# Where three of four value projections stand in the two attention stages with sixteen small heads

## The chip, the core and the metric

The kernel runs on one core of a Trainium2 chip. The core has a matrix engine (PE, or TensorE; the loading of its weights is shown as PEld), a vector engine (DVE), a scalar engine with tables for functions such as the exponential (ACT), a general engine (POOL) and a queue that issues transfers (SP). The engines run side by side, each through its own list of instructions in order, and wait for one another by semaphores. TensorE's clock is not constant: the profile shows which share of full speed was granted at each moment, called PEclk or granted clock. Matmuls write to PSUM, which this kernel divides into banks of 512 columns.

The metric is the time of one execution on the device in microseconds (us). Before the change it was 3802.96 us, the median of three runs (3797.84 to 3808.43).

## The reference

The program is a stack of four blocks on one activation of 2048 tokens by 128 features. Each block is half a feed-forward, an attention, and half a feed-forward again, all with a layer norm before and a residual after. The change touches the attentions of the second and the third block, which have sixteen heads of eight features and no causal mask; the third differs by a rotation of queries and keys:

```python
qkv = qkv.reshape(B, N, 3, HEADS, HEAD_DIM)        # 16 heads of 8
q, k, v = (qkv[:, :, 0], qkv[:, :, 1], qkv[:, :, 2])
q = q * scale
attn = jnp.einsum('bnhd,bmhd->bhnm', q, k)
attn = jax.nn.softmax(attn, axis=-1)
out = jnp.einsum('bhnm,bmhd->bnhd', attn, v)
```

With one batch of 2048 tokens each head has 2048 by 2048 scores. The values v of a token are its normed features times a matrix of 128 by 128.

## The kernel before, in words

**Tiling.** The 2048 tokens are four chunks (NC = 4) of 512 columns (CH), a chunk is four tiles (TC = 4) of 128. The function `packed` (line 1296) does one attention with small heads. The sixteen heads are four groups g of four; an iteration is a pair of a group and a chunk of queries, so there are sixteen, in the order group by group. The four heads of a group lie on the 128 partitions, 32 for each, so that a score product has 32 rows, and a value product 32 columns of output.

**Two passes.** The function `flash` (line 970) runs two streams. `stream_a` is the first pass: for an iteration it multiplies queries by all keys (line 1069) and takes the maximum of each row on DVE (line 1087, two heads at a time). It goes over the keys in two halves (`pi`, called `pair` in the hook): the chunks 0 and 1, then 2 and 3; in each over the four query tiles `r`. `stream_b` is the second pass: for each of the sixteen key tiles `kt` of 128 and each of the four heads it computes the scores again with the maximum folded in (line 1190), takes the exponential on ACT (line 1199), and multiplies by the values (line 1136) into one bank `pv`. The first pass of the first iteration runs alone; after that the two are interleaved in proportion to their columns, the first pass about one iteration ahead. The order on PE in these streams is fixed in the program by `tc.keep_in_program_order`; what is issued without it (projections, copies) is placed by a scheduler, earlier where it can, and `tc.high_priority()` lets it go ahead of others.

**Projections.** `front(c)` (line 1316) norms and turns a chunk and leaves it, turned, in `vall[c]`. `queries_or_keys(n, c)` (line 1325) makes keys (n = 1) or queries (n = 0) with three products of 512 columns (`product`, lines 227 to 229), cast on ACT and completed on DVE. `values(c)` (line 1334) multiplies the four tiles of `vall[c]` by the value matrix into one bank and copies that back into `vall[c]` on ACT (line 1341). It takes its bank from `bank()`, which has three, shared with the scores of the second pass and with the other projections.

**Stacks.** `stack_q` and `stack_k` put queries and keys of a group and chunk into their partitions by three DMAs each (line 1379), issued by SP. `stack_v(g, c)` (line 1401) copies the four heads' values of a chunk into the tile `v` of the group on DVE (line 1403); the value products read that tile. Key tile `kt` needs chunk `kt // 4`.

**Who calls what, and when.** `hook(n, pair, r)` is called by the first pass ahead of each query tile. For the first iteration it makes the last keys (pair 0, tile 0), and in the second half of the keys (`pair == 1`) it calls `values(r)` and `stack_v(0, r)` for r = 0 to 3, and at r = 2 stacks the queries of the second iteration. `poll(at)` is called in the second pass ahead of each of its steps, with the iteration and key tile at hand (-1 and 0 before the first). It stacks keys and values of group 1 at its first call, and later groups when an iteration has been passed. In the program's list for PE the scheduler has put the value projections of the second block's attention ahead of the first maximum's matmul, and those of the third block's among the first ones.

Of the kernel before, what the change touches and what calls it, by code (L numbers as in the profile page):

```python
# [21 lines left out]
NC = 4  # L22
# [42 lines left out]
def tile_macaron(ctx: ExitStack, tc: tile.TileContext, a: dict, out: bass.AP, stages=STAGES):  # L65
    nc = tc.nc
# [6 lines left out]
    def bank(name="bank"):  # L73
        return psum.tile([P, CH], F32, name=name, tag="s2", bufs=3)
# [1221 lines left out]
    def packed(io, early, hd, causal, scale, project, w, wv, wo, bias=None):  # L1296
# [4 lines left out]
        n_groups = C // (4 * hd)  # L1301
# [3 lines left out]
        def slots(v):  # L1305
            return v[:, : NT * 4 * slot].rearrange("p (t j d) -> p t j d", j=4, d=slot)
# [24 lines left out]
            last_of[n, c] = nc.vector.tensor_tensor(l, src, h.bitcast(F32), ALU.subtract)  # L1331
            parts[c][n] = h, l

        def values(c):
            ps = bank().rearrange("p (i c) -> p i c", i=TC)
            f = vall[c].rearrange("p i c -> p (i c)")
            for i in range(TC):
                nc.tensor.matmul(
                    ps[:, i], f[:, i * P : (i + 1) * P], wv, start=True, stop=True
                )  # L1340
            nc.scalar.copy(vall[c], ps)

        for c in range(1 if causal else NC - 1):
            while not io.ready(c):
                yield 0
            front(c)
            yield 1.5
            queries_or_keys(1, c)
            if c == 0:
                queries_or_keys(0, c)  # L1350
            yield 1.5
            if causal:
                values(c)
        yield True

        with tc.tile_pool(name="att", bufs=1) as pool, tc.tile_pool(name="far", bufs=1) as far:
# [27 lines left out]
            def stack_k(g, c):  # L1384
                t = kms[(g * NC + c) % n_km if not causal else g * NC + c]
                h, l = parts[c][1]
                for i in range(nq):
                    rows_of(t[:, i, :], (h, l, h), (g * nq + i) * per * hd)
                km[g, c] = t
# [11 lines left out]
            def stack_v(g, c):  # L1401
                vt[g] = vts[g % 2]
                nc.vector.tensor_copy(
                    slots(vt[g])[:, c * TC : (c + 1) * TC, :, :hd],
                    vall[c][:, :, g * 4 * hd : (g + 1) * 4 * hd].rearrange(
                        "p i (j d) -> p i j d", j=4
                    ),
                )
# [9 lines left out]
            def steps_of(i):  # L1418

                if not x_parts[i]:  # L1420
                    xn = layer_norm(i, False)
                    yield
                    front(i, xn)
                    yield
                    queries_or_keys(1, i)
                    if causal:
                        queries_or_keys(0, i)
                        yield
                        values(i)
                        yield  # L1430
                for g in range(2 if causal else 1):
                    stack_k(g, i)
                    if causal:
                        stack_v(g, i)
                        queue(its.index((g, i)))
                        yield

            def onward(c):

                if keyed[0] > c:  # L1440
                    return False
                if not making:
                    making.append(steps_of(keyed[0]))
                if next(making[0], True):
                    making.pop()
                    keyed[0] += 1
                return True
# [3 lines left out]
            def ensure(c):  # L1451
                while onward(c):
                    pass

            def queue(n):

                if n < len(its) and its[n] not in qt:
                    c = its[n][1]
                    if not parts[c][0]:
                        queries_or_keys(0, c)  # L1460
                    stack_q(*its[n])
# [8 lines left out]
            def hook(n, pair, r):  # L1470

                if causal:
                    if its[n][1] + 1 < NC:
                        onward(its[n][1] + 1)
                    return None
                if n == 0:
                    if pair == 0 and r == 0:
                        with tc.high_priority():
                            ensure(NC - 1)
                    if pair == 1:  # L1480
                        values(r)
                        stack_v(0, r)
                        if r == 2:
                            with tc.high_priority():
                                queue(1)
                elif pair == 1 and r == 2:
                    queue(n + 1)

                if n == 0 and (pair, r) in ((0, 1), (1, 3)):
                    return last_of[(1, NC - 1) if pair == 0 else (0, 1)]  # L1490
# [14 lines left out]
                    fill(t[:, NT * 4 * slot :], 1.0, True)  # L1505

            grown = [0 if not causal else n_groups]

            def poll(at):

                if causal:
                    return
                n, kt = at
                g = grown[0] + 1
                if g < n_groups and (g < 2 or n >= NC * (g - 1)):
                    for c in range(NC):
                        stack_k(g, c)
                        stack_v(g, c)
                    grown[0] = g
# [45 lines left out]
            def finish(n, pv, after, pe):  # L1565
# [32 lines left out]
                def out_b(oT):  # L1598
# [11 lines left out]

            io.upcoming()
            flash(io, pool, early, its, 4, causal, scale, s1, s2, pv_mm, put_max, begin, finish, poll,
                  leads=leads, hook=hook, flush=not causal, order=(2, 3, 0, 1) if per == 4 else (1, 0, 3, 2))

    def projections(pool, wqk):
# [24 lines left out]
    def attn0(io, k, w, early):  # L1640
        w, project = w
        yield from packed(io, early, 16, True, 16.0**-0.5, project, w, 2 * C, 3 * C)
# [5 lines left out]
    def attn1(io, k, w, early):  # L1648
        w, project = w
        yield from packed(io, early, 8, False, 8.0**-0.5, project, w, 2 * C, 3 * C, row("b_proj"))  # L1650
# [40 lines left out]
    def attn2(io, k, w, early):  # L1691
        w, project = w
        yield from packed(io, early, 8, False, 8.0**-0.5, project, w, 4 * C, 5 * C)
# [591 lines left out]
```

## Time and profile before

One execution was profiled. It took 3781.83 us, with a span of 3779.9 us from its first to its last instruction; the three runs shown above were executed without a profile.

| | busy us | share of the span |
|---|---|---|
| PE | 3450.8 | 91% |
| PEld | 1847.3 | 49% |
| DVE | 2873.0 | 76% |
| ACT | 2035.4 | 54% |
| POOL | 827.9 | 22% |

A busy engine is one with an instruction under way, whatever its clock. By windows around the two stages:

| from, to (us) | what runs | PE busy | DVE busy | ACT busy | granted clock |
|---|---|---|---|---|---|
| 802 to 866 | second block: front, and maxima of the first iteration | 37.54 | 52.62 | 7.41 | 0.58 |
| 866 to 915 | its second pass begins | 47.32 | 27.68 | 26.22 | 0.50 |
| 915 to 1600 | the rest of it | 666.96 | 617.37 | 555.12 | 1.00 |
| 1735 to 1782 | third block: maxima of the first iteration | 32.77 | 45.82 | 3.48 | 0.61 |
| 1782 to 1833 | its second pass begins | 49.32 | 29.78 | 26.47 | 0.50 |
| 1833 to 2450 | the rest of it | 593.71 | 567.36 | 531.78 | 0.98 |

In the profile a matmul of `values` stands as two passes of 128 columns each (line 1338: 32 passes for the sixteen matmuls of a stage). They start between 812.5 and 818.7 us in the second block and between 1735.4 and 1742.7 us in the third.

### The profile page before, as it was taken

To read this page: it belongs to the slowest core of one execution; us is meant where nothing else is said; L and a number is where in the kernel's file an instruction comes from. 1 tells how busy PE (TensorE), PEld (TensorE's weight loads), DVE (VectorE), ACT (ScalarE), POOL (GpSimd) and SP (SyncE) were. 2 spreads that over 40 slices of the span, in tenths; PEclk is the share of its full clock that TensorE was granted. 3 is DMA by queue.
4 is the path that set the end of the run, shared out by engine and by line. 5 is a ranking of instruction groups with operands and counts; after the bars stand their busy time and mean duration, and the time that the engine had idled before them with its cause. 6 is when DMAs were issued, how large, how long until landed. Compare 5 with 4: busy or idle time off the path is not lost. (4 is left out here: it accounts for less than half of the span.)

```text
span 3779.9 us, 64635 instructions
## 1 busy us (share of the span) xinstructions
PE 3450.8 (91%) x25325; PEld 1847.3 (49%) x25325; DVE 2873.0 (76%) x4793; ACT 2035.4 (54%) x3838; POOL 827.9 (22%) x830
## 2 busy tenths in 40 slices
PE   7689988979999999996999999988899999999999
PEld 5543356853333333883333333376444444444458
DVE  6578556767999997668799999654677877788862
ACT  3246722315888888332688888732333444444442
POOL 1511124010000000111000000142555445533341
PEclk9779989976999999996799999898899999999999
DMA  3410023010000000102000000012443333221010
GB/s 104 94 48 19 27 69 92 1 26 5 14 10 14 8 3 1 35 7 64 9 14 6 16 5 4 12 49 75 137 147 111 99 108 97 89 63 52 24 34 12
DMA packets 124689, 170.18 MB, mean 45 GB/s; under 512 B 25120, under 2 KB 52514, under 8 KB 124384
## 3 DMA queue, kind: packets, MB, share of 16 engines
q1 hardware_dynamic: 121824, 160.80, 14.0%
q0 software_dynamic: 2560, 5.25, 0.9%
q8 instruction: 199, 3.26, 0.4%
q14 instruction: 106, 0.87, 0.1%
HBM read 101.25 MB, written 45.87 MB: 39 GB/s over the span
## 5 line engine op out<-in xcount | busy, mean ns | idle before, releaser
L1087 DVE TENSOR_REDUCE mp<-s 128x2 f32<-128x1024 f32 (+3 forms) x1440 | 1628.1, 1181 | 115.3 <-PE s L1069 84.8
L1199 ACT ACTIVATE pt<-s 128x512 f32<-128x512 f32 (+1 forms) x2368 | 1220.4, 602 | 250.5 <-PE s L1190 155.5
L1190 PE MATMUL s<-q,km 32*128 32x512 f32 (+2 forms) x2368 | 751.9, 504 | 24.2 <-ACT pt L1199 14.2
L1136 PE MATMUL pv<-pt,v 128*32 128x256 f32 (+1 forms) x8568 | 752.6, 424 | 22.9 <-ACT ov L1568 11.3
L1069 PE MATMUL s<-km,qt 32*128 32x512 f32 (+3 forms) x2368 | 634.0, 519 | 57.5 <-DVE mp L1087 36.1
L1190 PEld LDWEIGHTS s<-q,km 32*128 32x128 f32 (+1 forms) x2368 | 329.7, 188 | 549.3 <-issue 360.6
L1179 ACT ACTIVATE pt<-s 128x512 f32<-128x512 f32 (+3 forms) x640 | 306.1, 530 | 357.0 <-PE s L1171 213.8
L143 POOL TENSOR_TENSOR rs<-rs,minus_half 128x4 f32<-128x4 f32 x56 | 57.7, 1030 | 1555.9 <-DVE rs L142 1555.0
L1136 PEld LDWEIGHTS pv<-pt,v 128*32 128x32 f32 x8568 | 171.1, 109 | 325.0 <-issue 151.8
L1984 DVE TENSOR_TENSOR sum<-sum,pt 128x512 f32<-128x512 f32 (+3 forms) x328 | 259.3, 806 | 89.0 <-ACT pt L1179 87.7
L1171 PE MATMUL s<-q,k 64*128 64x512 f32 (+3 forms) x1920 | 299.9, 403 | 16.3 <-ACT pt L1179 10.8
L1136 PE MATMUL pv<-pt,latv 128*64 128x512 f32 (+3 forms) x1280 | 310.7, 565 | 1.3 <-ACT pt L1179 1.3
L1984 POOL TENSOR_TENSOR sum<-sum,pt 128x512 f32<-128x512 f32 (+1 forms) x200 | 264.8, 1324 | 182.7 <-ACT pt L1179 179.6
L1069 PEld LDWEIGHTS s<-km,qt 32*128 32x128 f32 (+1 forms) x2368 | 241.0, 195 | 119.4 <-DVE mp L1087 79.2
L1171 PEld LDWEIGHTS s<-q,k 64*128 64x128 f32 x1920 | 161.7, 188 | 226.7 <-issue 138.3
L715 ACT ACTIVATE sg<-pg 128x1024 f32<-128x1024 f32 x72 | 73.9, 1026 | 174.3 <-PE pg L229 155.3
L1069 PE MATMUL s<-k,q 64*128 64x512 f32 (+3 forms) x640 | 132.4, 428 | 19.4 <-DVE mp L1087 19.0
L1782 DVE TENSOR_TENSOR rot<-rot,tab 128x512 f32<-128x512 f32 x128 | 87.7, 685 | 74.0 <-PE rot L229 39.4
L725 PEld LDWEIGHTS pd<-l1d,h 128*128 128x128 f32 x1152 | 139.3, 192 | 5.6
L725 PE MATMUL pd<-l1d,h 128*128 128x128 f32 x1152 | 140.1, 275 | 0.0
L717 DVE TENSOR_TENSOR h<-pu,sg 128x1024 f32<-128x1024 f32 x72 | 87.9, 1220 | 60.5 <-PE pu L229 55.5
L1171 PE MATMUL s<-q,two 64*128 64x512 f32 (+3 forms) x640 | 128.3, 369 | 0.0
(575 smaller groups left out, 4682.1 us busy)
## 6 DMA issues: line engine op xcount, KB each, us to landing
tab<-in_l3rope SPq DMA_DIRECT2D x66, 256.0 KB
q<-q SPq DMA_DIRECT2D x32, 512.0 KB
k<-k SPq DMA_DIRECT2D x32, 512.0 KB
l0e<-in_l0e SPq DMA_DIRECT2D x32, 256.0 KB
q<-h SPq DMA_DIRECT2D x32, 256.0 KB
q<-rot SPq DMA_DIRECT2D x32, 256.0 KB
k<-h SPq DMA_DIRECT2D x32, 256.0 KB
k<-rot SPq DMA_DIRECT2D x32, 256.0 KB
```

The source lines that it names most:

```text
L715: nc.scalar.activation(sg, pg, AF.Silu)
L717: nc.vector.tensor_tensor(h.rearrange("p m n -> p (m n)"), pu, sg, ALU.mult)
L725: nc.tensor.matmul(pd[:, i, :], h[:, m, i * P : (i + 1) * P], wd[:, m, :], start=m == 0, stop=m == 1,)
L1069: pe(nc.tensor.matmul(ps[:, o : o + w], lhsT, rhs[:, :w], start=True, stop=not masked))
L1087: ins = nc.vector.tensor_reduce(mp[:, r, j0 : j0 + 2, kc], both[:, :, :w], AX.X, ALU.max,)
L1136: i = pe(nc.tensor.matmul(pv[out_rows, lo:hi], lhsT, pts[j][:, lo:hi], start=kt == 0, stop=kt == nt - 1 and hi == CH))
L1171: pe(nc.tensor.matmul(outs[j][:, c0:], lhsT, rhs[:, c0:], start=i == 0, stop=i == len(terms[0]) - 1 and not diag,))
L1179: ex = nc.scalar.activation(pts[j][:, c0:], outs[j][:, c0:], AF.Exp, scale=scale)
L1190: pe(nc.tensor.matmul(ps[:, c0:], lhsT, rhs[:, c0:], start=i == 0, stop=i == len(terms) - 1 and (tiled or not diag),))
L1199: ex = nc.scalar.activation(pt[:, c0:], ps[:, c0:], AF.Exp, scale=scale)
L1782: nc.vector.tensor_tensor(t.bitcast(F32), ps, halves["tabs"][i], ALU.mult)
L1984: eng.tensor_tensor(t[:, c0:], other[:, c0:], pts[j][:, c0:], ALU.add)
```

## The change

`hook` calls `values` and `stack_v` for chunk 0 alone. `poll` gets a new condition: the first time that it is called in the first iteration with a key tile above 0, it makes the values of chunks 1, 2 and 3 and stacks them for group 0, with high priority, and with the matmuls kept in the program's order (`values` has a new argument for that). A list `dense` notes that this is done, and group 1 is stacked only afterwards. The causal attention of the first block goes through the same functions, but its calls of `values` are as before.

```diff
-        def values(c):
+        def values(c, keep=lambda ins: ins):
...
-                nc.tensor.matmul(
+                keep(nc.tensor.matmul(
                     ps[:, i], f[:, i * P : (i + 1) * P], wv, start=True, stop=True
-                )
+                ))
...
                     if pair == 1:
-                        values(r)
-                        stack_v(0, r)
+                        if r == 0:
+                            values(0)
+                            stack_v(0, 0)
...
             grown = [0 if not causal else n_groups]
+            dense = []
...
                 n, kt = at
+                if not dense and n == 0 and kt > 0:
+
+                    dense.append(n)
+                    with tc.high_priority():
+                        for c in range(1, NC):
+                            values(c, tc.keep_in_program_order)
+                            stack_v(0, c)
                 g = grown[0] + 1
-                if g < n_groups and (g < 2 or n >= NC * (g - 1)):
+                if g < n_groups and dense and (g < 2 or n >= NC * (g - 1)):
```

In the program's lists of instructions the twelve matmuls of chunks 1 to 3 then stand, in both stages, in one piece among the first score products of key tile 1: after one of them and a pair of the second iteration's maxima, and ahead of the next score product and of the first value product. Their three copies stand on ACT between exponentials, and six copies into `v` (chunks 1 to 3 for groups 0 and 1) on DVE between maxima. One matmul of chunk 0 stands behind the Q projection in the second block's front where it stood ahead of it. The DMAs of the keys and queries are the same; two of those at the start change places.

## What the change does to the time: a prediction

> **What bounds the kernel now.** I read the page's busy shares first (PE 91% of the span, DVE 76%), then the slices in time, then the two stages with sixteen heads by windows, then single instructions there. The change touches only those stages (about 802 to 1600 us and 1700 to 2450 us), so I need what limits them, and where. In the slices, compare the busy TensorE with the clock it was granted: in slices 10 and 20 PE is busy nine tenths while PEclk has 9 and 7.
>
> ```profile
> PE   7689988979999999996999999988899999999999
> PEclk9779989976999999996799999898899999999999
> ```
>
> The windows of the first of the two stages split that up. Columns: stretch, its length, busy us (instructions) of PE, PEld, DVE, ACT, POOL, then the granted clock.
>
> ```profile
> 820.00:860.00 40.00, 25.32 (x66) 9.22 (x66) 36.09 (x33) 0.00 (x0) 0.00 (x0) 0.53 0.13 33
> 866.00:880.00 14.00, 12.32 (x62) 3.95 (x60) 7.92 (x7) 9.06 (x16) 0.00 (x0) 0.50 0.00 0
> 880.00:890.00 10.00, 10.00 (x64) 3.02 (x60) 5.43 (x5) 4.14 (x8) 0.00 (x0) 0.50 0.01 2
> 890.00:900.00 10.00, 10.00 (x58) 3.10 (x52) 5.83 (x6) 5.10 (x10) 0.00 (x0) 0.50 0.00 1
> 900.00:920.00 20.00, 19.99 (x136) 6.48 (x135) 13.31 (x12) 12.25 (x24) 0.00 (x0) 0.63 0.04 11
> 920.00:960.00 40.00, 39.19 (x396) 15.63 (x396) 38.07 (x39) 35.14 (x68) 0.00 (x0) 1.00 0.05 11
> ```
>
> Three regimes: until about 866 the maxima of the first iteration run alone and DVE is full (36.09 of 40); from 866 the second pass runs on a full PE at **half clock**, with DVE and ACT about half idle; from about 915 the clock is 1.0 and PE and DVE are both full. The pace is read from the value products (L1136), two halves for each key tile:
>
> ```profile
> 883.35 1.08 PE L1136 MATMUL pv<-pt,v 128*32 128x256 f32 x8
> 885.09 1.08 PE L1136 MATMUL pv<-pt,v 128*32 128x256 f32 x8
> 887.62 1.08 PE L1136 MATMUL pv<-pt,v 128*32 128x256 f32 x8
> ...
> 915.45 0.64 PE L1136 MATMUL pv<-pt,v 128*32 128x256 f32 x8
> 916.74 0.64 PE L1136 MATMUL pv<-pt,v 128*32 128x256 f32 x8
> 917.75 0.64 PE L1136 MATMUL pv<-pt,v 128*32 128x256 f32 x8
> ```
>
> At half clock a key tile takes 887.62 - 883.35 = 4.27 us, at full clock 917.75 - 915.45 = 2.30 us. The second stage repeats it: clock 0.50 from 1748, full pace from 1833.19. So for some 45 us of each stage the bound is the granted clock, and the question is **what raises it**. In this trace every step of the clock lies a whole number of 3.413 us apart from every other (805.7, 815.95, 822.8, 914.9), so it is decided window by window. In the second pass windows full of score and value products are refused twelve times; the rise at 914.9 comes one window after a Q projection (L227 to L229, 128 rows, 908.23 to 909.9), the one at 1833.1 two windows after another (1824.33 to 1827.2). After both, the halves follow at 1.74 us steadily, where 1.74 and 2.53 us alternated before. And just such value projections as are moved here have raised it, before the maxima:
>
> ```profile
> 812.00:813.00 1.00, 1.00 (x4) 0.91 (x5) 0.57 (x1) 0.40 (x1) 0.00 (x0) 0.50 0.00 0
> 813.00:814.00 1.00, 1.00 (x6) 1.00 (x6) 0.00 (x0) 0.19 (x1) 0.00 (x0) 0.50 0.00 0
> 814.00:815.00 1.00, 1.00 (x4) 0.81 (x4) 0.00 (x0) 0.13 (x1) 0.00 (x0) 0.50 0.00 0
> 815.00:816.00 1.00, 1.00 (x7) 1.00 (x6) 0.52 (x1) 0.94 (x2) 0.00 (x0) 0.53 0.00 0
> 816.00:817.00 1.00, 1.00 (x10) 1.00 (x10) 0.44 (x3) 0.42 (x1) 0.00 (x0) 1.00 0.25 61
> ```
>
> Within the window 812.5 to 815.95 lie two K products and some twelve value passes; at its end the clock is 1.0. In the second stage the window 1734.1 to 1737.5, mostly value passes, ends in a rise too.
>
> **What is removed from the front.** Per stage twelve of the sixteen matmuls of `values` go; the trace has two passes for each, so 24 passes, with 3 copies on ACT (585 ns each, L1341) and 6 on DVE (L1403, median 218 ns: three for group 0, three for group 1, whose stacking now waits for the new place too). In the first stage 14 passes (814.63 to 816.74) stand ahead of the Q projection of chunk 1 on PE. That is on the path, through SP's queue: the rest of the first query tile (`qt<-qL`, issued at 820.81) is queued behind the tile of chunk 1, which waits for the cast of that projection (ACT, 817.72 to 818.30); the first maximum's matmul starts at 823.16. With the passes gone the cast ends about 2.07 us earlier (816.23). But SP had issued two of the key copies (815.48, 816.20) while it waited, and in the new order they come after it, before `qt<-qL`: from 816.25, six issues of 0.47 to 0.6 us put it at 819.8, **1.0 us earlier**. The other key and query DMAs keep their order. In the second stage DVE carries the front from 1735.49 to 1783: the hole at 1737.85 to 1738.70, in which the reduction waits for a score matmul behind value passes (0.85 us), goes, and about 0.9 us of DVE copies between the maxima: **1.7 us**.
>
> **What is added at the second pass.** The new order of PE puts the 24 passes after the second iteration's score pair at 869.49 (before), ahead of the fourth score matmul of key tile 1 and the first value product. Each projection takes one of the three banks that the scores use, and waits for the exponential that frees it; ACT runs its first exponentials from 868.35 at some 0.51 us each, so the third is done at 869.9 and the fifth at 870.9, before their banks are wanted. Queued behind the burst on PE are a score matmul, which waits for the first projection's ACT copy (done while the other two run), and the value product. On ACT the three copies stand ahead of the next exponential, on DVE the six copies ahead of the next maxima, for up to 0.6 us after the burst, when their next inputs are not there. I cost the DVE copies at 0.6 us a stage, half of 6 x 0.2: nothing if the idle DVE hides them (5.4 busy of 10 before), 1.2 if DVE is already the bound.
>
> The price of the burst: cold, six passes took 1.14 us (812.49 to 813.63), 0.19 each, so 24 take 4.6 us; at full clock some 0.10 each (14 passes in 2.11 us, the clock rising among them). By the windows above, about 1 us of value passes in a window besides score products should carry it over: the rise then falls 1 to 4.4 us after the burst's start, as the window happens to lie; I take 2.6 us (14 passes cold, 10 warm): **3.6 us**. Ends: 2.9 us; and 4.6 us plus up to 3.3 us at the cold pace of 3.48 us a tile, if a second window is needed (another 1.1 us lost).
>
> **What it brings.** First stage, from 869.98 to 915.01, 45.0 us before: the value product of key tile 0 (2.58 us cold, 1.4 warm), 19 halves, one Q projection. At full clock: 1.4 + 19 x 1.15 = 21.85 + Q 0.8 (its warm length at 816.74) + burst 3.6 = 27.65. Gain **17.4 us**. Second stage, 1786.08 to 1833.19, 47.1 us: the same 19 halves, a projection of six products (1.55 warm, 1739.06 to 1740.6): 1.4 + 21.85 + 1.55 + 3.6 = 28.4. Gain **18.7 us**. Sum: 17.4 + 18.7 + 1.0 + 1.7 - 1.2 = 37.6, say **37 us**. What is late next is DVE, 98% full at full clock; that is in the 2.30 us.
>
> [...]
>
> **Against the median.** The profiled execution took 3781.83 us (span 3779.9), the median of three is 3802.96, and none was under 3797.84. The sum is made within the profile: 3745. I keep the 21 us between the two, since nothing here says where they lie: 3766. If the timed runs find their rise later than the profiled one, the gain is larger.
>
> **Rivals.**
> 1. *One stage only.* The burst lifts one stage, and in the other the windows cut it so that it counts too little, or a quiet window drops the clock again (as once at 1874, for one window). For: windows with half a projection were refused (908.1, 1822.9). Against: these held 128x512 products, and the window at 812.5 rose with less. Gain about 37 - 19 = 18: 3785.
> 2. *The clock doesn't rise at the burst* and rises at the Q projection as before: front -2.7, burst +9.1, copies +1.2, about +8: 3811; less where the steady 1.74 us comes earlier (3.48 against 4.27 a tile). With that it is no measurable change.
> 3. *Slower: the old trigger is lost as well.* The rise in the second pass is narrow: windows nearly as full as the one at 911.5 were refused (887.6). If the burst fails and shifts the streams so that the Q projection no longer tips it, the clock stays at half until the next iteration's projection, 16 tiles x 1.97 us = 31 us in a stage: 3803 + 8 + 31 = 3842. It decides when the clock is still 0.50 after the projection of query chunk 2.
>
> That the moves aren't made is excluded by the order of the instructions; the rest of the program keeps its order but for one table load and one rotation in the front of the second stage.
>
> **Chances.** Forecast 0.74 (3748 to 3778 by the ends above), one stage only 0.12, no rise 0.08, lost trigger 0.06. 0.3% is 11.4 us, what a measurement of this kernel can tell from no change. Faster: 0.74 + 0.12 = 0.86; same 0.08; slower 0.06. The range 3742 to 3800 takes in the first two cases, and at the low end timed runs in which the old rise was later.
>
> **What would show it.** In the profile after: granted clock 1.0 within about 5 us of the twelve projections in both stages, the halves of L1136 1.15 us apart from the second key tile on, the first maximum's matmul 1 us earlier in the first stage, no L1341 between the maxima of the second. It is wrong if the clock stays 0.50 through the burst, or falls again within the first iteration.

## The result, and the profile after

The changed kernel takes 3765.32 us (median of five, 3762.61 to 3769.46), the kernel before 3802.96: 0.990 of it, with a 95% interval of 0.9881 to 0.9919. In a later comparison it was 0.9913 (0.9892 to 0.9934). The profiled execution took 3769.46 us. The forecast of 3766 was met; the sum behind it was not, as the stages show.

The slices of the page, busy TensorE and granted clock (against the two rows of before: slice 10 has PEclk 7 for 6, where the prediction's text has 9, and slice 20 has 9 for 7):

```profile
PE   7679987978999999996999999888999999999989
PEclk9779988987999999996999999998899999999999
```

The first stage by windows (length, then busy us of PE, PEld, DVE, ACT, POOL, granted clock). This execution reaches the stage 13 us later than the first profile did; its second pass begins at about 882:

```profile
820.00:880.00 60.00, 34.89 (x97) 15.07 (x97) 49.56 (x49) 3.59 (x8) 5.33 (x10) 0.53 0.12 32
882.00:887.00 5.00, 4.59 (x20) 3.95 (x21) 2.58 (x4) 2.91 (x6) 0.00 (x0) 0.50 0.01 3
887.00:914.00 27.00, 24.18 (x217) 9.00 (x217) 20.71 (x21) 19.14 (x37) 0.00 (x0) 1.00 0.00 1
914.00:960.00 46.00, 45.22 (x450) 18.28 (x449) 43.22 (x43) 40.54 (x78) 0.00 (x0) 1.00 0.06 14
```

The half clock ends at 887.2, some 5 us into the second pass, where it lasted 47 us before; in the second stage it ends at 1795.2. But from 887 to 914 PE is busy only 24.18 of 27 us, DVE 20.71, ACT 19.14: at full clock no engine is full. PE in order of time shows the burst and what follows:

```profile
883.63 4.66 PE L1338 MATMUL bank<-l1a,vall 128*128 128x128 f32 x24
...
888.64 1.06 PE L1136 MATMUL pv<-pt,v 128*32 128x512 f32 x8
...
892.32 0.64 PE L1136 MATMUL pv<-pt,v 128*32 128x256 f32 x8
892.89 0.50 PE L1190 MATMUL s<-q,km 32*128 32x512 f32 x1
892.90 0.50 PE L1069 MATMUL s<-km,qt 32*128 32x512 f32 x2
893.69 0.50 PE L1190 MATMUL s<-q,km 32*128 32x512 f32 x1 [0.29 <-ACT pt L1199]
894.18 0.64 PE L1136 MATMUL pv<-pt,v 128*32 128x256 f32 x8
...
895.18 0.64 PE L1136 MATMUL pv<-pt,v 128*32 128x256 f32 x8
```

The burst starts at 883.63, and the clock rises 3.6 us later. After it the halves follow at 1.86 and 1.01 us by turns (892.32, 894.18, 895.18), so 2.86 us for a key tile and not 2.30; in front of every second one a score matmul waits for an exponential. That lasts for eight tiles, until the Q projection at 913.7. The waits of ACT in that time (engine and line, for whom, us in total, times, longest), first after, then in the kernel before from 873 to 908:

```profile
ACT pt L1199 <- PE pv L1136: 6.4, 8, 0.8
```

```profile
ACT pt L1199 <- PE pv L1136: 17.6, 8, 2.2
```

The same eight waits stand in both (and in the second stage, 6.3 us after and 17.6 before): an exponential waits for a **value product**. It writes a tile `pt`, and waits until an older one has been read. No row shown in the prediction had this wait, and its sum has no term for it.

By stages, the time from the first exponential of the second pass to the last value product:

| | before, two profiles | after, two profiles |
|---|---|---|
| second block | 649.1, 650.3 | 640.3, 639.1 |
| third block | 663.4, 665.3 | 648.7, 653.5 |
| sum | 1312.5, 1315.6 | 1289.0, 1292.5 |

The stages gain 23 us on average, where the prediction had 36.1 without the fronts and 34.9 with its reserve for DVE.

### The profile page after: what moved, and what is told of

The parts are those of the page before. It is cut to its first block, busy times and chain, and to the rows that moved or that the text cites. A ratio compares the mean times of both kernels' runs of the same rounds, so it can differ in the third digit from the quotient of the medians.

```text
span 3767.7 us, 64628 instructions
## 1 busy us (share of the span) xinstructions
PE 3420.8 (91%) x25325; PEld 1846.5 (49%) x25325; DVE 2870.9 (76%) x4793; ACT 2036.2 (54%) x3838; POOL 828.8 (22%) x830
## 5 line engine op out<-in xcount | busy, mean ns | idle before, releaser
L1190 PE MATMUL s<-q,km 32*128 32x512 f32 (+2 forms) x2368 | 733.6, 491 | 28.6 <-ACT pt L1199 18.7
L1136 PE MATMUL pv<-pt,v 128*32 128x256 f32 (+1 forms) x8568 | 730.9, 413 | 22.9 <-ACT ov L1577 11.2
L1069 PE MATMUL s<-km,qt 32*128 32x512 f32 (+3 forms) x2368 | 620.0, 507 | 61.1 <-DVE mp L1087 37.1
```

The costliest lines, as they stand in the source:

```text
L1069: pe(nc.tensor.matmul(ps[:, o : o + w], lhsT, rhs[:, :w], start=True, stop=not masked))
L1136: i = pe(nc.tensor.matmul(pv[out_rows, lo:hi], lhsT, pts[j][:, lo:hi], start=kt == 0, stop=kt == nt - 1 and hi == CH))
L1190: pe(nc.tensor.matmul(ps[:, c0:], lhsT, rhs[:, c0:], start=i == 0, stop=i == len(terms) - 1 and (tiled or not diag),))
```

## The experiments

The theories when they began. **A**: the burst of full-array products raises the clock, and that is the gain. **B**: the emptier fronts and the moved copies are the gain. Later, from the waits of ACT, **C**: the second pass is short of tiles for the exponentials. Ratios are to the kernel before on the same chip.

**The kernel before, again.** No edit.

> The kernel before, unchanged, with a second profile and five more timed runs. Theory A (the half clock at the start of the second passes is what the change removes, and its length differs from run to run): the times spread between 3782 and 3808, the longer ones have a lower mean granted clock, and the profile has half-clock stretches of at least 85 us around the start of each second pass. Rival (the half-clock stretch is the same in every run, and the 21 us between the profiled run and the median are elsewhere): the stretches end with the Q projection of the third query chunk again, and times don't follow the mean clock.

Ratio 1.000 (0.9985 to 1.0015); 22 executions from 3779.59 to 3819.32 us, with the mean clock going against the time (correlation -0.93): 0.938 in the shortest, 0.927 in the longest. So times do follow the clock, as A has it. But the second profile has its stretches of half clock in the same places, ending after the Q projections, and took 3799.9 us. It differs from the first profile ahead of the touched stages: its first attention begins at 193.7 us against 185.3, and from that attention's end to the next one's start it is another 6.7 us. These 15 us go with the chip, not the kernel: on the two chips where the kernel before has a median of 3781 or 3786 that start is at 184 to 189 us and the second stretch 363 us long, on the two with 3803 or 3804 it is 193 to 196 and 369 to 371, for every version run here. Part of it is a pause of TensorE among the gathered products, 5.0 us in the one feed-forward and 6.5 in the other, which the first profile doesn't have; what causes it is open. The record doesn't name the chip of the first profile, but by its start it goes with the faster two. So most of the 21 us between that profile and the median was probably the chip, and keeping them in the forecast was right.

**The burst alone.** The values stay in the front; the same twelve products are made a second time at the second key tile and not read:

```diff
+                if not burst and n == 0 and kt > 0:
+                    burst.append(n)
+                    with tc.high_priority():
+                        for c in range(1, NC):
+                            ps = bank("burst")
+                            for i in range(TC):
+                                tc.keep_in_program_order(nc.tensor.matmul(
+                                    ps[:, i * P : (i + 1) * P], vall[c][:, i, :], wv, start=True, stop=True
+                                ))
```

> The value projections stay in the front as before; a copy of the burst alone is added at the second key tile: twelve matmuls of 128x128 whose result nobody reads. Theory A (the burst raises the clock, and the clock is the gain): granted clock 1.0 within 5 us of the burst in both stages, about 34 us faster than before (the 37 less the 2.7 of the fronts), so 3765 to 3775. Rival B (the emptier fronts and the moved copies are the gain): slower than before by the burst, 6 to 9 us, near 3810.

Ratio 0.9932 (0.9912 to 0.9952), 28 us faster than before, though it does more. Its windows around the burst, which starts at 885.99:

```profile
884.00:889.00 5.00, 4.31 (x20) 3.59 (x19) 2.45 (x2) 2.67 (x6) 0.00 (x0) 0.50 0.00 0
889.00:915.00 26.00, 23.44 (x217) 8.61 (x216) 19.19 (x17) 17.12 (x33) 0.00 (x0) 1.00 0.00 1
```

The clock is 1.00 from 889, and B is out as the main cause: most of the gain needs nothing moved.

**A burst of another kind.** As above, with products of 32 rows in place of the full ones:

```diff
-                                    ps[:, i * P : (i + 1) * P], vall[c][:, i, :], wv, start=True, stop=True
+                                    ps, qt[its[0]][rows(0), 0, i * P : (i + 1) * P],
+                                    km[0, 0][rows(0), 0, :], start=True, stop=True
```

> The kernel before with a burst of the same place and about the same length (12 products of 512 columns, some 5 us at half clock), but of 32 rows by 128 columns each, one after another, result unread. Theory A (what counts in a window is how much of the array works): the clock stays 0.50 through the burst and comes with the Q projection as before; the time is that of before plus the two bursts, 3803 to 3815. Rival (a window in which TensorE has no gap is enough, whatever it does): the clock rises within 5 us of the burst as in the run with full products, 3770 to 3780.

Ratio 1.0013 (0.9999 to 1.0028). PE and its windows:

```profile
869.09 4.10 PE L1521 MATMUL burst<-km,qt 32*128 32x512 f32 x9
872.57 0.79 PE L1190 MATMUL s<-q,km 32*128 32x512 f32 x1
872.99 1.48 PE L1521 MATMUL burst<-km,qt 32*128 32x512 f32 x3
```

```profile
868.00:875.00 7.00, 6.99 (x21) 4.56 (x25) 1.81 (x2) 2.38 (x5) 0.00 (x0) 0.50 0.00 0
875.00:911.00 36.00, 35.69 (x204) 10.34 (x196) 20.27 (x17) 16.72 (x33) 0.00 (x0) 0.50 0.00 1
```

PE is busy 6.99 of 7 us, for longer than the full burst, and the clock stays at 0.50 for 46 us more, to 920.6. So a PE without gaps was not enough here: behind 4.37 us of full products the clock was 1.00 from 889, behind 5.58 us of 32-row products it was 0.50. The two bursts also differ in width (128 columns at a time against 512), but behind products of 128 rows and 512 columns it rose too, at 871.1 in the early Q projections below.

**Not in one piece.** Eight passes each at key tiles 1, 5 and 9; group 1 is stacked after the third:

```diff
-                if not dense and n == 0 and kt > 0:
+                c = len(dense) + 1
+                if c < NC and n == 0 and kt >= 4 * c - 3:
...
```

> The same move, but a chunk at a time: eight passes at key tile 1, eight at key tile 5, eight at key tile 9. Theory A with the weight I put on a projection (1 us of value passes in a window is enough): the first eight passes, 1.5 us, raise the clock in about half of the windows' positions, so between the kernels: 3765 to 3790. Theory A2 (a window must be nearly full of projections): the clock stays 0.50 until the Q projection and the time is near that of before, 3795 to 3810. Rival B (front): as after, 3765.

Ratio 0.997 (0.9953 to 0.9988), 13 executions from 3777.75 to 3803.20, so between the kernels and wide. In its one profile the eight passes at 884.03 sufficed in the first stage (clock up at 887.8); in the second those at 1792.45, 1811.32 and 1830.39 did not, and it came at 1840.1, after the Q projection. Three windows of the clock, found from its steps, hold of the value passes (length, then busy us of PE and PEld with L1338 alone, granted clock):

```profile
884.37:887.78 3.41, 1.74 (x8) 1.44 (x7) 0.50 0.02 5
1792.31:1795.73 3.42, 2.08 (x8) 1.78 (x8) 0.50 0.02 5
1829.86:1833.27 3.41, 2.07 (x8) 1.78 (x8) 0.50 0.00 0
```

```profile
1796.00:1836.00 40.00, 39.75 (x221) 14.04 (x213) 21.28 (x21) 17.95 (x34) 0.00 (x0) 0.50 0.00 0
```

The first of these windows ended in a rise; the other two did not, though all eight passes lay in them. So the clock rose behind a burst of 2.1 us once and not the other times; what decided it is open. Behind the piece of 24 passes it rose in both stages of the profile after (4.66 and 5.28 us of passes, up at 887.2 and 1795.2), and in the first stages of the burst alone (4.37 us, 1.00 from 889), of the earlier burst (4.63 us from 880.97, with the next score product at 0.50 us) and of the version with the Q projections below (0.91 on average from 872 to 880). My "about 1 us of value passes in a window is enough" is refuted at 1792.

**A tile earlier.** The burst ahead of the last scores of key tile 0:

```diff
-                if not dense and n == 0 and kt > 0:
+                if not dense and n == 0:
```

> The burst one key tile earlier, ahead of the last scores of key tile 0. Theory A: the clock rises some 2 us earlier, and what runs between is at full speed 1 to 2 us a stage sooner: 2 to 4 us faster than after. Rival (the burst then holds up the first exponentials and their values, and the start waits): the same as after or up to 4 us slower.

Ratio 0.9919 (0.9899 to 0.9939), where the change has 0.990 and 0.9913: no gain that can be told. The second passes take 639.0 and 653.8 us, as in the two profiles after.

**More tiles.** The waits of ACT named value products. The tag `pt` has ten tiles, and the normed inputs of a chunk (`xH`, `xL`, line 1294) are allotted from the same ten, until the chunk's queries are made. Chunks 2 and 3 hold four of them when the second pass begins. With three more, in the kernel before (line 1178, which is like 1198, is edited too):

```diff
-        return lambda dt, name: early.tile([P, CH], dt, name=name, tag="pt", bufs=10)
+        return lambda dt, name: early.tile([P, CH], dt, name=name, tag="pt", bufs=13)
...
-                        pt = early.tile([P, CH], F32, name="pt", tag="pt", bufs=2 * nh + 2)
+                        pt = early.tile([P, CH], F32, name="pt", tag="pt", bufs=13 if nh == 4 else 2 * nh + 2)
```

> The kernel before with 13 tiles of the tag pt in place of 10, in the attentions with small heads. Theory C (the normed inputs of chunks 2 and 3 hold four of the ten tiles that the exponentials write, until their queries are made; with six left the second pass alternates 1.74 and 2.53 us, and with the steady 1.74 us the windows are full enough for the clock): steady 1.74 us from the second key tile on, clock 1.0 within 10 us of the second pass's start, and then 2.30 us a tile, with no burst at all: 25 to 45 us faster than before, 3758 to 3778. Rival D (the Q projection's own dense products lift the clock, and the tiles are not short): alternating pace and half clock until 45 us into the pass, as before, 3795 to 3810.

Ratio 0.9895 (0.9872 to 0.9918), with no burst at all. ACT's wait for value products is gone; what it waits for from 870 to 885 is:

```profile
ACT pt L1199 <- PE s L1190: 2.2, 2, 2.0
ACT pt L1199 <- PE s L1069: 0.6, 4, 0.2
```

The pace is 2.24 us a tile from the first tile at full clock, and the clock rose at 872.4 and 1770.1, some 5 and 11 us into the passes. So the short tiles are what made the pace alternate. That the steady pace by itself raises the clock seemed settled too, until the second profile of the same kernel:

> The kernel before with 13 tiles of the tag pt once more, for a second profile and a second chip. The change with 13 tiles stood at 0.985 of before, the kernel before with 13 tiles at 0.990, on different chips. Theory C (the burst adds nothing once the tiles are there): 0.983 to 0.990, and the second passes of the two stages together within 10 us of the 1271 us of the change with 13 tiles. Rival (the burst still brings a gain of its own): 0.990 again, and 1280 us or more.

Ratio 0.9895 again (0.9868 to 0.9921), on another chip. In the first stage:

```profile
868.00:890.00 22.00, 21.75 (x144) 5.91 (x136) 14.68 (x13) 12.99 (x25) 0.00 (x0) 0.50 0.00 1
890.00:915.00 25.00, 25.00 (x163) 7.51 (x159) 16.57 (x15) 14.88 (x28) 0.00 (x0) 0.50 0.04 9
915.00:925.00 10.00, 9.53 (x89) 3.57 (x89) 8.52 (x11) 7.89 (x16) 0.00 (x0) 0.81 0.09 21
```

```profile
871.74 1.08 PE L1136 MATMUL pv<-pt,v 128*32 128x256 f32 x8
873.48 1.08 PE L1136 MATMUL pv<-pt,v 128*32 128x256 f32 x8
875.22 1.08 PE L1136 MATMUL pv<-pt,v 128*32 128x256 f32 x8
```

Steady 1.74 us, and half clock until 918.8, over the Q projection at 899.57 too; in the second stage the clock rose at 1785.7. Theory C holds for the pace, and not for the clock: with enough tiles it comes soon in one execution and 50 us late in another, and the steady pace at half clock (3.48 us a tile against 4.27) is what is sure. The value products don't tell which: in the first execution the 3.41 us before the rise at 872.4 held 1.94 us of them, in the second the clock stayed at 0.50 to 915 with 1.08 us of them in every 1.74. A tile at half clock (3.48 us) and the spacing of the clock's steps (3.41) differ by 0.07 us, so that the products drift slowly against the steps; that this is why one position can last is my reading, not shown.

**The Q projections early.** In the kernel before those of chunks 2 and 3 at the second key tile, which frees the four tiles and is dense as well:

```diff
+                if not asked and n == 0 and kt > 0:
+                    asked.append(n)
+                    with tc.high_priority():
+                        for c in range(2, NC):
+                            queries_or_keys(0, c)
```

> The kernel before with the Q projections of chunks 2 and 3 already at the second key tile, in one piece (six products of 512 columns in the first stage, twelve in the second); nothing else moved. Theory C: both free tiles and are dense; the clock rises within 7 us of them, and 2.30 us a tile at once: 3758 to 3775. Theory D gives the rise too, but 2.86 us a tile until the old place: 3768 to 3785. If the burst of values is needed: 3795 or more.

Ratio 0.9898 (0.9875 to 0.9921). The clock rises within 4 us of the first projection in the first stage (at 871.1), and the halves are steady at full clock, 2.30 us a tile:

```profile
873.64 0.64 PE L1136 MATMUL pv<-pt,v 128*32 128x256 f32 x8
874.64 0.64 PE L1136 MATMUL pv<-pt,v 128*32 128x256 f32 x8
875.94 0.64 PE L1136 MATMUL pv<-pt,v 128*32 128x256 f32 x8
```

The rise came before the second key tile, in a window with 2.51 us of projections, so the freed tiles had no part in it. This is the wait and the clock cured without moving a value projection, to the same gain as the change within the intervals; its two second passes take 1275.9 us together.

**The change and the Q projections.**

```diff
                             stack_v(0, c)
+                        for c in range(2, NC):
+                            queries_or_keys(0, c)
```

> The changed kernel with the Q projections of chunks 2 and 3 right behind the burst of values. Theory C: after the burst the halves of a tile follow at 1.15 us at once, where the changed kernel had 2.86 us a tile for eight tiles: 4 to 5 us less in each stage, 3753 to 3760. Rival (the 2.86 us come from the cold start of the streams, not from tiles): the same as the changed kernel, 3763 to 3768.

The pace does become 2.30 us a tile (halves 1.00 and 1.29), so the 2.86 were the tiles. The ratio, 0.9906 (0.9887 to 0.9926), doesn't tell it from the change alone; its second passes take 635.3 and 650.4 us, 4 less than after in the first stage and 1 in the second. The second had one more stretch of half clock, 17 us at 1935.

**The changed kernel, again.** No edit.

> The changed kernel, unchanged, on the chip of the other runs of this call. Theory C predicts no new number: about 1% under before, half clock until some 5 us into the second passes, then 2.86 us a tile until the Q projection of chunk 2. If the second passes of the two stages take 1289 us together again (before: 1313 and 1316 in two profiles), some 26 us of the difference to before are the stages' and the rest is run-to-run difference of the others.

The ratio of 0.9913 above; 1292.5 us for the second passes. The first attention took 249.6 us in this profile and 246.4 in the other of the same kernel, so the 3 us there are chance and not the change's.

**The change with 13 tiles.** Both edits.

> The change together with 13 tiles of the tag pt. Theory C: the tiles already give the steady pace and so the clock; the burst then only adds its own 3 to 5 us a stage and saves 1 to 3 us in the fronts: within 6 us of the kernel before with 13 tiles, either way. Rival (the burst and the tiles are two separate gains): another 15 to 25 us less than with either alone.

Ratio 0.9846 (0.9824 to 0.9869): lower than 13 tiles alone on their two chips (0.9895 both), by some 18 us, though the intervals all but touch. The profiles go the same way against one of those two and not the other (1271.5 us for the second passes against 1266.6 and 1285.5). With 13 tiles alone the clock rose in the first stage at 872.4 in one execution and at 918.8 in the other; with the burst it came at 886.0 and 1783.7, each within 7 us of the second pass's start. So the two are neither one gain, as I expected, nor a sum.

**13 tiles and the early Q projections.**

> The kernel before with 13 tiles and the Q projections of chunks 2 and 3 at the second key tile. Theory C: both ways free the same exponentials, so hardly more than one of them; the clock may come a window sooner in the second stage, which had half clock for 11 us there: 0 to 8 us less than with 13 tiles alone. Rival: the sum of both, some 75 us under before.

Ratio 0.9819 (0.9797 to 0.9841), 3735.62 us: the fastest version of the study, 36 us under the changed kernel on the same chip (3771.88), with 1254.2 us for the second passes. I had expected 0 to 8 us less than with 13 tiles alone; by the ratios (0.9895 there) it is some 29. Its pace at full clock from the first tile:

```profile
897.38 0.64 PE L1136 MATMUL pv<-pt,v 128*32 128x256 f32 x8
898.38 0.64 PE L1136 MATMUL pv<-pt,v 128*32 128x256 f32 x8
899.61 0.64 PE L1136 MATMUL pv<-pt,v 128*32 128x256 f32 x8
```

## Why the prediction was right, and where its sum was not

- *The bound: half clock at the start of the second passes.* Right: the burst alone, with everything else left in place, gave 28 us.
- *The value projections raise the clock where full windows of score and value products were refused.* Right, and now shown: behind a burst of full products the clock was 1.00 from 889, behind one of 32-row products, 5.58 us against 4.37, TensorE was busy 35.69 of 36 us at 0.50.
- *The price of the burst*, 3.6 us. It took 4.66 us in the first stage and 5.28 in the second, since the clock rose only 3.6 and 4.9 us after its start and not 2.6. The mis-sized term is how much of the projections in a window was taken to suffice: 1 us, where 2.08 us were not enough at 1792 in the spread version. The rows of before spoke against it: the window that ended at 815.95, which I took to have risen with less than half a projection, held full-array products throughout, 2.76 us of value passes among them, while those at 908.1 and 1822.9 were refused. Cost: 1.1 and 1.7 us.
- *The pace at full clock, 2.30 us a tile.* This is the step that failed. I took it from after the Q projection of the old trace, and named DVE as what is late next. What was late next was ACT, for tiles: 2.86 us, 8 tiles a stage, 4.5 us in each. The alternation of 1.74 and 2.53 us stood in my own text, and I read it as a sign of the clock only; what ACT waited for in those 35 us (17.6 us, for value products) gives the cause, and a change as good as this one.
- *The fronts*, 1.0 and 1.7 us. From the first transposes to the first maximum's matmul the first stage took 13.05 and 13.15 us before, 12.36 and 12.75 after: 0.5 on average. From the first maximum to the second pass the third block took 49.8 and 48.7 before, 48.0 and 49.0 after: 0.7 on average, within the spread of the profiles.
- *The old trigger.* I held the Q projection's own density to be what tipped the clock. It also freed tiles, and the steady pace that followed was fuller. Which of the two tipped it is not separated: at 1845.0 in the second profile of before the rise ended a window with 2.2 us of the projection, at 914.9 one that held none; with 13 tiles the pace was steady from the start and the clock came soon in three of four stages, and in the fourth neither the pace nor the projection tipped it.
- *The sum.* In the profiles the stages gain about 23 us and the fronts 1.3, together some 25 of the predicted 37. The terms above account for the rest: 9 us of pace, 2.8 of bursts, 1.4 of fronts. The timed runs gain 38 (31 to 45) in the first comparison and 33 (25 to 41) in the second. Part of the distance is which executions were profiled: the two of the changed kernel are 4 and 3 us above the medians beside them, the second one of before is 2 below. What is left is open. Executions of the kernel before went down to a mean clock of 0.924, where its two profiles have 0.934 and 0.932; where those lost it no profile shows. So the mechanism was right, and that the time fell on 3766 is in part luck: the sum is 12 us too large against the profiles, and the timed runs gained more than the profiles.
- *The signs and rivals.* The clock rose within 5 us of the burst's start in both stages, as forecast; the halves did not follow at 1.15 us. One of the named signs of being wrong came once: in the second profile after, in the third block, the clock fell again within the first iteration, from 1827.0 to 1833.8, behind a window in which TensorE was busy for 2.47 of 3.41 us. None of the rivals came; "One stage only" describes the spread version, at 0.997.

## What to carry to other kernels

Where an engine is full at half clock, ask two things apart: what would raise the clock (here, 24 full-array passes in one piece, 4.66 and 5.28 us), and why the stream is not denser by itself. The second was the cheaper cure: inputs that wait for a later use held four of the ten tiles that the exponentials turn over, and three more tiles, or using those inputs up sooner, each gave as much as the moved projections (0.9895 and 0.9898 against 0.990). A forecast that takes its pace from a later part of the trace should check that the waits of that part are the same.

## What the runs showed of the hardware

In the profile before every step of the granted clock lies a whole number of 3.413 us from every other (805.7, 815.95, 822.8 and 914.9 among them), and in the profile after as well. Cut at these distances, the two profiles have windows at different places of the program: in the third block's second pass the first boundary behind the first score product comes 2.15 us after its start before (1783.19 to 1785.34) and 1.21 us after it in the changed kernel (1787.15 to 1788.36). The same program had half clock for 5 us after the start of a second pass in one execution (13 tiles, to 872.4) and for 53 us in another (to 918.8).

A TensorE without gaps was not enough to raise the clock: with a burst of 32-row products it was busy 6.99 of 7 us at 0.50, and in the kernel before 20.00 of 20 us from 880 to 900. In the profile after, the two windows that were filled by the 24 passes, 3.41 us each, both ended in a rise (887.2 and 1795.2). With less of them, or of the Q projection, windows ended either way: 1.74 us and a rise, 2.08 and none (the spread version), 2.51 and a rise (the early Q projections), 1.97 and none, none at all and a rise (before, at 1826.3 and 914.9).

The first attention began at 184 to 189 us on the two chips where the kernel before has a median of 3781 or 3786 us, and at 193 to 196 on the two with 3803 or 3804, and the second stretch was 363 us long on the former and 369 to 371 on the latter, for every version run here. So a profile and the timed runs beside it should come from one chip before their difference is read.
